# Gating moved to VectorE between the convolution's halves, state products on four column tiles, transposes placed behind halves of the step products

## The chip, the cores and the metric

The program runs on one core of a Trainium2 chip. The time is the device time of one execution in microseconds (us), as the median of several executions. Five engines work side by side and meet through semaphores: TensorE (PE in the profile; PEld is its weight load), VectorE (DVE), ScalarE (ACT), GpSimd (POOL), and SyncE (SP), which issues the DMAs. Each engine takes its own instructions strictly in order.

## The reference

The whole program is a decoder of six layers over x, 8 sequences of 256 tokens with 256 features: x = layernorm(x + layer(x)) six times. The change touches only the first layer, a gated convolution (called `mamba` in the code), and nothing of what it computes:

```python
def _L0_attn_ref(x, W_in, conv_w, conv_b, W_xproj, D, W_out):   # D_STATE = 16
    d_inner, d_conv = conv_w.shape                # 512, 4
    xz = einsum('bld,ed->ble', x, W_in)           # 1024 columns
    xb, z = xz[..., :d_inner], xz[..., d_inner:]
    xpad = pad(xb, d_conv - 1 in front)
    xc = conv_b
    for k in range(d_conv):
        xc = xc + conv_w[:, k] * xpad[:, k:k + L, :]
    xc = silu(xc)
    proj = einsum('bld,ed->ble', xc, W_xproj)     # 16 + 16 + 512 columns
    Bm, Cm = proj[..., :16], proj[..., 16:32]
    delta = softplus(proj[..., 32:])
    bc = einsum('bls,bls->bl', Bm, Cm)
    y = delta * xc * bc[..., None] + D * xc
    y = y * silu(z)
    return einsum('bld,ed->ble', y, W_out)
x = layernorm(x + _L0_attn_ref(...))
```

All data are float32.

## The kernel before

The 2048 tokens are cut into four groups of 512 (two sequences each), numbered by `s`. Inside the layer the features lie on the 128 partitions and the 512 tokens along the free dimension; the 512 inner channels are four chunks of 128, handled in pairs (`c2` is the pair, `c` the chunk). A pair fills one `pair` buffer of PSUM, 128 x 1024 values, two banks. There are three `pair` buffers and two one-bank buffers called `one`.

The functions of one group, in the words of the layer:

- `turn_in(s)`: eight 128x128 transposes of x on PE into two `one` buffers (L88), each copied to SBUF by ACT (L93).
- `project(s)`: four `pair` buffers of four matmuls each (L172). The first two pairs are the channels xb: ACT copies each into the padded tile `xp` (L183), DVE makes the convolution with eight instructions a pair (L187 twice, L192 six times), ACT applies Silu and leaves `xc` (L197). The last two pairs are z: ACT applies Silu from PSUM and leaves `sz` (L178).
- `state(s)`: four matmuls add W_bc's products for the 32 columns B and C into 32 partitions of a `one` buffer (L207). DVE shifts B onto C and multiplies (L212, L214).
- `state_sums`: one matmul with ones adds the 16 products and spreads the sum over all 128 partitions (L219); ACT copies it to `bc` (L221).
- `steps(s, c2)`: eight matmuls (L229) make softplus's argument for one pair; ACT applies Abs (L234) and Exp (L235). `gated` adds ACT's Ln (L240), then DVE takes max(ps, 0) + e (L242), POOL multiplies by `bc` (L243), DVE adds D and multiplies by xc (L246, twice), POOL multiplies by `sz` (L249). The result is `y`. Each of Exp, Ln and Silu is preceded by a load of ACT's function table where it follows another.
- `outputs(s, half, o)`: eight matmuls of y with W_out into a `one` buffer (L259), then the residual sum and layernorm of 256 tokens (`norm`: DVE L103, L110, L111, two small POOL instructions, DVE L116).
- `turn_out(s, half, ps)`: four transposes of the layer's result and ACT's copy (L88, L93), input of the next layer.

The recording layer puts instructions into each engine's order; `tc.issue_after(x)` holds those recorded inside it until after x. A PSUM or SBUF buffer is given to a new tile when its last reader is done. In the order that results, PE's work for one group in the middle is: `state`, `turn_in(s+1)` mixed with the first steps, `steps(s, 0)`, `state_sums`, `steps(s, 1)`, `project(s+1)`, `outputs(s)`, and from s = 1 `turn_out(s-1)` before or in the middle of the next group's first products. After the last `steps` PE goes straight on with the second layer (`cross`), whose first functions are `values` (L342) and `weighted_values` (L361): their PSUM results are copied alternately by ACT (L74) and DVE (L76), and the layer's remaining `outputs(3)` and `turn_out` calls are spread between them.

The loop over the groups:

```python
            for s in range(4):
                bc_p = state(s)
                if s + 1 < 4:
                    turn_in(s + 1)
                e0 = steps(s, 0)
                bc = state_sums(bc_p)
                e1 = steps(s, 1)
                gated(s, 0, *e0, bc)
                gated(s, 1, *e1, bc)
                if s + 1 < 4:
                    last = project(s + 1)
```

## Time and profile before

| what | us | from |
|---|---|---|
| median of three executions | 1465.47 (1463.72 to 1466.76) | times |
| the profiled execution, time | 1460.47 | times |
| the profiled execution, span of its instructions | 1458.0 | page |
| PE busy in the span | 1379.0 (95%) | page, part 1 |
| DVE, ACT, POOL busy | 834.5 (57%), 654.9 (45%), 522.4 (36%) | page, part 1 |
| first layer, PE: first transpose to last step product | 3.72 to 178.6 | timeline of PE |
| PE, DVE, ACT, POOL busy in the first 180 us | 164.8, 87.8, 80.9, 42.3 | table of windows of 20 us |

The matmul records of float32 come in two for each instruction (the timeline shows x16 for eight matmuls of `steps`), so "x16" of L229 in 7.0 us means 0.88 us an instruction. Durations of one engine's successive instructions overlap a little where they do not depend on each other, so sums are best taken from start to start. In the timeline the number in brackets is the engine's idle time before the row, and behind the arrow stands what released it.

### The profile page before, as it was taken

How to read it: one execution, taken by the hardware profiler on the slowest of the kernel's cores; microseconds unless marked ns; L12 is line 12 of the kernel's file. 1: busy time of each engine (PE TensorE's matmuls, PEld its weight loads, DVE VectorE, ACT ScalarE, POOL GpSimd, SP SyncE). 2: the span in 40 equal slices, each digit the busy share in tenths (PEclk: the TensorE clock that was granted, in tenths of full speed). 3: DMA queues.
4: the chain of work that ended last, by engine and by line, in shares of the span. 5: the costliest groups of instructions: out<-in, count | busy, mean ns of one | idle time of the engine just before them, and what ended most of it. 6: DMA issues, size and time to landing. Idle time of an engine off the chain costs nothing.

```text
span 1458.0 us, 21959 instructions
## 1 busy us (share of the span) xinstructions
PE 1379.0 (95%) x7938; PEld 963.7 (66%) x7938; DVE 834.5 (57%) x2285; ACT 654.9 (45%) x1608; POOL 522.4 (36%) x525
## 2 busy tenths in 40 slices
PE   8999889999999999999989999999999999899996
PEld 3443468888885666656566666678888787566564
DVE  3654435564662523323658888835555662787886
ACT  3555342333332112221248877833333322877884
POOL 0333122222210113317435666432343455556541
PEclk9999999999999999999999999999999999999999
DMA  9100023324360012233030000024222210000100
GB/s 236 34 0 1 0 93 93 107 70 156 115 229 15 19 40 87 87 105 105 29 102 1 1 1 2 1 90 123 74 73 82 82 35 9 16 16 16 30 16 16
DMA packets 71679, 87.81 MB, mean 60 GB/s; under 512 B 5588, under 2 KB 66164, under 8 KB 71060
## 3 DMA queue, kind: packets, MB, share of 16 engines
q1 hardware_dynamic: 68164, 77.10, 17.3%
q0 software_dynamic: 3408, 9.31, 2.3%
q8 instruction: 64, 1.05, 0.3%
q14 instruction: 43, 0.35, 0.1%
HBM read 56.87 MB, written 29.52 MB: 59 GB/s over the span
## 4 chain that ended last, share of the span: by engine, by line
PE 75%; DVE 15%; ACT 4%; POOL 3%; issue 3%; DMA 0%; SPq 0%; POOLq 0%; DVEq 0%; ACTq 0%
PE mm L481 9%; PE sc L436 8%; PE mm L737 7%; DVE p L990 6%; PE mm L800 5%; PE op L1027 4%; PE tr L754 4%; PE ps_sc L1012 4%; PE pair L229 4%; PE ps_sc L981 4%; PE sc L399 2%; PE tr L814 2%; PE sc L417 2%; PE sc L465 2%; PE mm L342 2%
## 5 line engine op out<-in xcount | busy, mean ns | idle before, releaser
L997 ACT ACTIVATE p<-p,nmx 128x256 f32<-128x256 f32 x512 | 252.9, 495 | 64.1 <-DVE nmx L990 64.0
L456 POOL TENSOR_TENSOR p<-p,sm 128x616 f32<-128x616 f32 x60 | 72.6, 1216 | 247.4 <-DVE sm L453 217.0
L481 PE MATMUL mm<-Ub,pT 128*128 128x256 f32 (+1 forms) x640 | 144.6, 379 | 0.5 <-ACT pT L74 0.4
L436 PE MATMUL sc<-M,xT_s 128*128 128x308 f32 x512 | 139.6, 423 | 0.8 <-ACT pT L74 0.8
L1012 PE MATMUL ps_sc<-ident,p 128*128 128x128 f32 x1024 | 132.0, 276 | 7.6 <-DVE nmx L990 4.8
L1012 PEld LDWEIGHTS ps_sc<-ident,p 128*128 128x128 f32 x1024 | 113.4, 141 | 34.2 <-issue 13.1
L481 PEld LDWEIGHTS mm<-Ub,pT 128*128 128x128 f32 (+1 forms) x640 | 120.8, 190 | 20.0 <-ACT pT L74 0.9
L737 PE MATMUL mm<-xT_s,w 128*128 128x512 f32 x256 | 115.2, 603 | 2.9 <-DVE h L743 2.1
L436 PEld LDWEIGHTS sc<-M,xT_s 128*128 128x128 f32 x512 | 94.0, 188 | 33.4 <-ACT pT L74 1.5
L449 ACT ACTIVATE p<-p 128x616 f32<-128x616 f32 x64 | 45.8, 716 | 150.0 <-DVE p L445 128.5
L990 DVE CUSTOM_DVE_ANT_0 p<-ps_sc,zero 128x256 f32<-128x256 f32 x256 | 90.7, 421 | 27.6 <-PE ps_sc L981 26.0
L990 DVE CUSTOM_DVE_ANT_0 p<-ps_sc,term 128x256 f32<-128x256 f32 x256 | 90.7, 420 | 27.6 <-PE ps_sc L981 27.5
L997 ACT ACTIVATION_READ_ACCUMULATOR p<-p,nmx 128x1 f32 x512 | 95.8, 187 | 0.0
L774 POOL DMA_INDIRECT xb<-xd,token x39 | 37.2, 954 | 147.3 <-PE tr L781 81.1
L737 PEld LDWEIGHTS mm<-xT_s,w 128*128 128x128 f32 x256 | 48.4, 193 | 58.1 <-issue 53.9
L443 DVE TENSOR_REDUCE nmx<-sc 128x8 f32<-128x616 f32 x64 | 51.1, 799 | 54.2 <-PE sc L436 54.2
L1015 DVE COPY pT<-ps_sc 128x1024 f32<-128x1024 f32 x64 | 77.7, 1214 | 2.7 <-PE ps_sc L1012 2.7
L1015 ACT COPY pT<-ps_sc 128x1024 f32<-128x1024 f32 x64 | 63.7, 996 | 28.8 <-PE ps_sc L1012 28.7
L800 PE MATMUL mm<-wE,xbT 128*128 x156 | 73.5, 593 | 0.3 <-ACT xbT L786 0.3
L741 ACT ACTIVATE g<-mm 128x512 f32<-128x512 f32 x32 | 19.1, 597 | 103.5 <-PE mm L737 99.6
L1027 PE MATMUL op<-pT,va 128*32 128x256 f32 x1024 | 63.4, 386 | 0.0
L452 DVE TENSOR_REDUCE sm<-p 128x8 f32<-128x616 f32 x64 | 50.6, 790 | 22.5 <-ACT p L449 21.9
(287 smaller groups left out, 2654.1 us busy)
## 6 DMA issues: line engine op xcount, KB each, us to landing
Ub<-ud SPq DMA_DIRECT2D x32, 512.0 KB
ud<-U SPq DMA_DIRECT2D x16, 616.0 KB
wE<-in_wE SPq DMA_DIRECT2D x4, 1536.0 KB
yd<-y SPq DMA_DIRECT2D x39, 128.0 KB
Ub<-ud SPq DMA_DIRECT2D x32, 104.0 KB
ud<-U SPq DMA_DIRECT2D x4, 608.0 KB
x_s<-in_x SPq DMA_DIRECT2D x8, 256.0 KB
w<-in_Wo SPq DMA_DIRECT2D x2, 1024.0 KB
```

Of the source, the lines that this page charges most:

```text
L229: nc.tensor.matmul(ps[:, i, :], w_dt[:, kc, c * P : (c + 1) * P], xc[s][kc // 2][:, kc % 2, :], start=kc == 0, stop=kc == 3,)
L436: nc.tensor.matmul(sc[:, a, : 4 * NCTX], xT_b[:, kc, j * P : (j + 1) * P], M[:, a * 4 : a * 4 + 4, kc, at : at + NCTX], start=kc == 0, sto ...
L456: engine.tensor_tensor(pv, pv, bcast(sm, 2, [P, 8, NCTX]), ALU.mult)
L481: nc.tensor.matmul(o[:, j * D : (j + 1) * D], pT[:n, c, j * P : (j + 1) * P],  Us[b][:n, g, c], start=g == 0 and j == 0 and c == 0, stop=g ...
L737: nc.tensor.matmul(ps, w[:, kc, cols], xT_s[:, kc, :], start=kc == 0, stop=kc == 1)
L754: nc.tensor.matmul(o[:, j * D : (j + 1) * D], hs[c][:, at : at + P], w3[:, c, :], start=c == 0, stop=c == 7,)
L800: nc.tensor.matmul(ps, xT[:, kc, :], column(j, kc * 512, 512), start=kc == 0, stop=kc == 1)
L990: self.last = nc.vector.tensor_tensor_reduce(out=p[:, h, :], in0=s4[:, h, :], in1=self.term(b, qb), scale=-1.0, scalar=3.0e38, op0=ALU.add ...
L997: nc.scalar.activation(p[:, h, :], p[:, h, :], AF.Exp, bias=nmx[:, qb, n : n + 1], scale=-1.0, accum_out=sums[:, qb, n : n + 1],)
L1012: nc.tensor.transpose(tr[:, at : at + P], p[:, h, kb * P : (kb + 1) * P], ident)
L1015: (nc.scalar.copy if j else nc.vector.tensor_copy)(self.pT[b, c, j][:, :, :, qb * P : (qb + 1) * P], tr.rearrange("p (h k t) -> p h k t", ...
L1027: nc.tensor.matmul(self.op[b][s * 32 : (s + 1) * 32, c, :], va[:, kb, 8 * c + 2 * s + m, :], self.pT[b, c, s // 2][:, s % 2 * 2 + m, kb, : ...
```

## The change

Four things are changed in the first layer.

1. `state` writes the four chunks' products side by side: each chunk's 32 columns go to a column tile of its own (`tile_position=(0, c * 32)`) and to 32 partitions of its own in half of a `pair` buffer, without adding. ACT copies the 128 x 512 result to `pt`, and a new matmul (`state_products`) with the constant `quarters` (ones where the partition's number modulo 32 is the column's) adds the four parts. The shuffle and the product follow as before, in place. `quarters` is made once by a reduction of the identity on DVE.
2. `gated` does its two multiplications, by `bc` and by `sz`, on DVE. POOL does none of the gating any more. The second pair's gating of group s is recorded inside `project(s + 1)`, between the two halves of the convolution: DVE's order is the first pair's gating, the copy and convolution of the first pair of s + 1, the second pair's gating, the convolution of the second pair.
3. The copy of the first pair into `xp` goes from ACT to DVE (L190); the second stays on ACT.
4. The order on PE: `steps` chains its halves with `issue_after`; `state_products` and `turn_in(s + 1)` come behind `steps(s, 0)`, the transposes between the first products of `steps(s, 1)`; `state_sums` comes between the halves of `steps(s, 1)`; `turn_out(s - 2)` (one group later than before) behind `steps(s, 1)`; `outputs(s)` behind `project(s + 1)`; `state(s + 1)` behind `outputs(s)`.

DMAs, their order on SP, and every engine's order behind the first layer stay as they are, but that `turn_out(1)` now stands right before the second layer's first product.

```diff
-            done, xc, sz, y = [], {}, {}, {}
+            done, xc, sz, y, bc = [], {}, {}, {}, {}
+            quarters = m1.tile([P, 32], F32, name="quarters")
+            nc.vector.tensor_reduce(
+                quarters, ident.rearrange("p (k m) -> p m k", k=4), AX.X, ALU.add
+            )
...
-                    nc.scalar.copy(xp[:, :, 3:], ps.rearrange("p i (b t) -> p (i b) t", b=2))
+                    copy = nc.scalar.copy if c2 else nc.vector.tensor_copy
+                    copy(xp[:, :, 3:], ps.rearrange("p i (b t) -> p (i b) t", b=2))
                     acc = m2.tile([P, 4, SEQ], F32, tag="acc", name="acc")
+                    order = ExitStack()
+                    if c2 == 1 and between:
+                        with tc.issue_after(conv.ins):
+                            order.enter_context(tc.issue_after(between().ins))
...
             def state(s):
-                ps = one()
+                parts = pair()[:, 0, :]
                 for c in range(4):
                     nc.tensor.matmul(
-                        ps[:32, :], w_bc[:, c, :], xc[s][c // 2][:, c % 2, :],
-                        start=c == 0, stop=c == 3,
-                    )
+                        parts[c * 32 : (c + 1) * 32, :], w_bc[:, c, :], xc[s][c // 2][:, c % 2, :],
+                        start=True, stop=True, tile_position=(0, c * 32),
+                    )
+                pt = m1.tile([P, 512], F32, tag="pt", name="pt")
+                nc.scalar.copy(pt, parts)
+                return pt
+
+            def state_products(pt):
+                ps = one()
+                nc.tensor.matmul(ps[:32, :], quarters, pt, start=True, stop=True)
                 sh = m1.tile([32, 512], F32, tag="sh", name="sh")
                 nc.vector.stream_shuffle(sh, ps[:32, :], [(i + 16) % 32 for i in range(32)])
-                bc_p = m1.tile([32, 512], F32, tag="bc_p", name="bc_p")
-                nc.vector.tensor_tensor(bc_p, ps[:32, :], sh, ALU.mult)
-                return bc_p
+                nc.vector.tensor_tensor(sh, ps[:32, :], sh, ALU.mult)
+                return sh
...
             def gated(...):
-                nc.gpsimd.tensor_tensor(t, t, bcast(bc, 1, [P, 2, 512]), ALU.mult)
+                nc.vector.tensor_tensor(t, t, bcast(bc[s], 1, [P, 2, 512]), ALU.mult)
...
-                nc.gpsimd.tensor_tensor(t, t, sz[s][c2], ALU.mult)
                 y.setdefault(s, []).append(t)
+                return nc.vector.tensor_tensor(t, t, sz[s][c2], ALU.mult)
...
             turn_in(0)
-            project(0)
+            last = project(0)
             for s in range(4):
-                bc_p = state(s)
-                if s + 1 < 4:
-                    turn_in(s + 1)
-                e0 = steps(s, 0)
-                bc = state_sums(bc_p)
-                e1 = steps(s, 1)
-                gated(s, 0, *e0, bc)
-                gated(s, 1, *e1, bc)
-                if s + 1 < 4:
-                    last = project(s + 1)
+                with tc.issue_after(last.ins):
+                    pt = state(s)
+                e0, last = steps(s, 0)
+                with tc.issue_after(last.ins):
+                    bc_p = state_products(pt)
+                    if s + 1 < 4:
+                        turn_in(s + 1)
+                e1, last = steps(s, 1, lambda: state_sums(s, bc_p))
+                if s > 1:
                     with tc.issue_after(last.ins):
                         for half in range(2):
-                            outputs(s, half, one())
-                        if s > 0:
-                            for half in range(2):
-                                turn_out(s - 1, half, one())
+                            turn_out(s - 2, half, one())
+                gated(s, 0, *e0)
+                if s + 1 == 4:
+                    gated(s, 1, *e1)
+                else:
+                    last = project(s + 1, lambda: gated(s, 1, *e1))
+                    with tc.issue_after(last.ins):
+                        for half in range(2):
+                            last = outputs(s, half, one())
```

More of the change, by code (lines that the diff above doesn't have):

```diff
@@ L162, in turn_in, with project @@
                     transposed(one(), x_s[:, half * 2 : half * 2 + 2, :], xT_s, half)
-            def project(s):
+            def project(s, between=None):
                 xT_s = xs[s][1]
@@ L191, in project @@
                         for k in range(1, 4):
-                            nc.vector.scalar_tensor_tensor(
+                            conv = nc.vector.scalar_tensor_tensor(
                                 acc[:, two], xp[:, two, k : k + SEQ], cv[:, c, k : k + 1],
@@ L195, in project @@
                             )
+                    order.close()
                     t = m2.tile([P, 2, 512], F32, tag="xc", name="xc", bufs=4)
@@ L214, in state, with state_sums @@
-                nc.vector.tensor_tensor(bc_p, ps[:32, :], sh, ALU.mult)
-                return bc_p
-            def state_sums(bc_p):
+                nc.vector.tensor_tensor(sh, ps[:32, :], sh, ALU.mult)
+                return sh
+            def state_sums(s, bc_p):
                 ps = one()
-                nc.tensor.matmul(ps, ones[:16, :], bc_p[:16, :], start=True, stop=True)
-                bc = m1.tile([P, 512], F32, tag="bc", name="bc")
-                nc.scalar.copy(bc, ps)
-                return bc
@@ L224, in steps @@
-            def steps(s, c2):
-                ps = pair()
+                last = nc.tensor.matmul(ps, ones[:16, :], bc_p[:16, :], start=True, stop=True)
+                bc[s] = m1.tile([P, 512], F32, tag="bc", name="bc")
+                nc.scalar.copy(bc[s], ps)
+                return last
+            def steps(s, c2, between=None):
+                ps, last = pair(), None
                 for i in range(2):
                     c = c2 * 2 + i
-                    for kc in range(4):
-                        nc.tensor.matmul(
-                            ps[:, i, :], w_dt[:, kc, c * P : (c + 1) * P],
-                            xc[s][kc // 2][:, kc % 2, :], start=kc == 0, stop=kc == 3,
-                        )
+                    with tc.issue_after(last.ins) if last else nullcontext():
+                        for kc in range(4):
+                            last = nc.tensor.matmul(
+                                ps[:, i, :], w_dt[:, kc, c * P : (c + 1) * P],
+                                xc[s][kc // 2][:, kc % 2, :], start=kc == 0, stop=kc == 3,
+                            )
+                    if i == 0 and between:
+                        with tc.issue_after(last.ins):
+                            last = between()
@@ L235, in steps, with gated @@
                 nc.scalar.activation(e, e, AF.Exp, scale=-1.0)
-                return ps, e
-            def gated(s, c2, ps, e, bc):
+                return (ps, e), last
+            def gated(s, c2, ps, e):
                 nc.scalar.activation(e, e, AF.Ln, bias=1.0)
@@ L258, in outputs @@
                         at = half * 256 + j * P
-                        nc.tensor.matmul(
+                        last = nc.tensor.matmul(
                             o[:, j * D : (j + 1) * D], y[s][c // 2][:, c % 2, at : at + P],
@@ L264, in outputs @@
                 norm(o, xs[s][0][:, two, :], n_s[:, two, :])
+                return last
             def turn_out(s, half, ps):
@@ L270, in mamba @@
             turn_in(0)
-            project(0)
+            last = project(0)
             for s in range(4):
-                bc_p = state(s)
-                if s + 1 < 4:
-                    turn_in(s + 1)
-                e0 = steps(s, 0)
-                bc = state_sums(bc_p)
-                e1 = steps(s, 1)
-                gated(s, 0, *e0, bc)
-                gated(s, 1, *e1, bc)
-                if s + 1 < 4:
-                    last = project(s + 1)
+                with tc.issue_after(last.ins):
[7 more added lines that the diff above has]
+                if s > 1:
                     with tc.issue_after(last.ins):
                         for half in range(2):
-                            outputs(s, half, one())
-                        if s > 0:
-                            for half in range(2):
-                                turn_out(s - 1, half, one())
+                            turn_out(s - 2, half, one())
[4 more added lines that the diff above has]
+                    last = project(s + 1, lambda: gated(s, 1, *e1))
+                    with tc.issue_after(last.ins):
+                        for half in range(2):
+                            last = outputs(s, half, one())
         return done, [
```

## The prediction

> **What bounds the kernel now.** I read the page first: PE is busy for 95% of the span and holds 75% of the chain that ended last, so a change pays if it takes work or waiting off PE, and costs if PE has to wait for what it moves to another engine. The change lies in the first layer, so I then read who waited for whom in the first 190 us (engine, line, whom it waited for: us in total, times, longest):

> ```profile
> PE one L88 <- DVE r L103: 7.5, 4, 2.0
> PE one L207 <- DVE r L103: 1.9, 1, 1.9
> PE pair L172 <- DVE y L242: 0.7, 3, 0.2
> DVE y L246 <- POOL y L243: 12.3, 5, 2.5
> ```

> PE's real waits inside the layer are for r, the residual sum that empties a `one` buffer of `outputs`: DVE is late with it, because the second half of a convolution and the gating stand before it. The timeline of PE shows where, for the last group (start, duration, row; in brackets the idle time before it and the releaser):

> ```profile
> 131.81 7.03 PE L172 MATMUL pair<-xT_s,w 128*128 128x512 f32 x16
> 139.09 7.13 PE L172 MATMUL pair<-xT_s,w 128*128 128x512 f32 x16 [0.25 <-DVE y L242]
> 146.06 7.07 PE L259 MATMUL one<-w,y 128*128 128x256 f32 x32
> 154.92 0.66 PE L88 MATMUL one<-ident,x_s 128*128 128x128 f32 x4 [1.79 <-DVE r L103]
> 155.41 1.02 PE L229 MATMUL pair<-xc,w 128*128 128x512 f32 x2
> 158.39 0.66 PE L88 MATMUL one<-ident,x_s 128*128 128x128 f32 x4 [1.96 <-DVE r L103]
> 158.98 5.32 PE L207 MATMUL one<-xc,w_bc 128*32 128x512 f32 x8
> 164.22 6.28 PE L229 MATMUL pair<-xc,w 128*128 128x512 f32 x14
> 170.43 1.12 PE L219 MATMUL one<-bc_p,ones 16*128 16x512 f32 x2
> 171.48 7.13 PE L229 MATMUL pair<-xc,w 128*128 128x512 f32 x16
> 178.45 3.74 PE L342 MATMUL mm<-ctxT,w 96*128 96x128 f32 x32
> 184.94 2.00 PE L361 MATMUL sc<-w,VT 64*128 64x256 f32 x16 [2.75 <-ACT VT L74]
> 190.20 3.50 PE L361 MATMUL sc<-w,VT 64*128 64x256 f32 x16 [3.26 <-DVE VT L76]
> ```

> The reader is to see three things. L207, `state`, takes four full-length matmuls for only 32 columns (3.5 us in the other groups). The two waits of nearly 2 us come right behind `outputs`. And L207 takes 5.3 us here: the table of windows gives PE's granted clock as 0.54 from 158.9 to 162.0, so these two waits also cost half speed for some 3.4 us, 1.7 us of work. At the end PE waits twice for the copies of VT, which stand behind the last gating.

> The rows that price the change (group rows: busy, mean ns of one | idle before; the last two are from the timeline of DVE):

> ```profile
> L1027 PE MATMUL op<-pT,va 128*32 128x256 f32 x1024 | 63.4, 386 | 0.0
> L1015 DVE COPY pT<-ps_sc 128x1024 f32<-128x1024 f32 x64 | 77.7, 1214 | 2.7 <-PE ps_sc L1012 2.7
> L456 DVE TENSOR_TENSOR p<-p,sm 128x616 f32<-128x616 f32 x4 | 3.2, 795 | 0.0
> 103.49 0.99 DVE L187 TENSOR_SCALAR acc<-xp,cv 128x512 f32<-128x512 f32 x2
> 104.40 4.05 DVE L192 SCALAR_TENSOR_TENSOR acc<-xp,cv,acc 128x512 f32<-128x512 f32 x6
> ```

> **State products (part 1).** L1027 already runs float32 products on four column tiles: 63.4 us for 1024 records of 256 columns, 62 ns each where one alone shows 386, and in the timeline 32 of them take 1.87 us to the next row. Eight records of 512 columns are half of that, 0.94; I take 1.0 against 3.53, start to start (66.54 to 70.07). [...] Saving 4 x 2.53 = 10.1 us. The new `quarters` matmul is one of L207's kind (3.53 / 4): 4 x 0.9 = 3.6 us on PE. Its input, ACT's copy of 128 x 512 (0.59 as L221), has the 7 us of `steps(s, 0)` to hide in; what follows it (shuffle and product 1.4 us on DVE) has the transposes and half of `steps(s, 1)`, 4.5 us, before `state_sums` asks. Making `quarters` is one small reduction while DVE idles until 13 us: nothing.

> **The waits behind `outputs` (part 4).** They go: now `state` writes a `pair` buffer, and the next `one` is asked for by `quarters`, 8 us after `outputs` end. From 43 us on the timeline lists 0.24, 1.88, 0.25, 1.78, 1.96, 0.25, 1.79, 1.96: 10.1 us, and the half clock at 159, 1.7 us. [...] The windows show the drop right behind them, so I count it. [...]

> What could be late instead: in the changed kernel's instruction order the third `pair` of `project` waits for DVE's new copy of the first, the fourth for ACT's copy of the second, `outputs` for the second gating, `state` for both halves of xc. I count from the end of the first `pair` of `project`, 0. DVE: copy 1.25 (L1015), convolution 4.9 (103.49 to 108.38), gating: max 1.25 (L242 has 1225 ns), multiply, two of L246 1.45 (row 1.42), multiply. The multiply has no row of its size; L456 gives 795 ns for 616 columns, L1015 1214 for 1024, L743 and L103 about 690 for 512, so 1.2 by the slope, 1.25 with hand-over; above, POOL's own 2.35. So gating is 5.2, ends 11.35; the second convolution ends at 16.3, Silu (1.06) at 17.4. PE: three more `pair`s of 3.5, at 10.5; three products of the first y are put first, so the second y is asked for at 11.8; `outputs` end at 17.5, half of `state` at 18.0, when the second xc is asked for. Both come about 0.5 early, and the third `pair` is asked for at 3.5, copy done at 1.3. Without that cover each us more on DVE in this chain is a us on PE, three times. I take no loss. ACT is given `pt` but loses one copy of 1.0 and is at 20 us of work in a round of 39: hidden. POOL keeps only memsets and the two small operations of `norm`; the DVE rows that ran beside it (L187 twice in 3.02 at 93.15, instead of 0.99) get their time back. `turn_in` and `turn_out` keep their numbers; SP and DMAs do not move, and the weights that are now asked for earlier (W_dt at 25 us instead of 28) are issued at 10 us (were they late, it is at most the 3 us, once).

> **The end of the layer.** From the last step product (178.5) to the second L361 is 11.7 us before. After: Abs, Exp, Ln and their two table loads 5.8, two `turn_out` copies that stand between them 1.2, last gating 5.2, copy of VT 0.7: 12.9. But two `turn_out`s of 0.5 have moved from before the last step product to behind it, under this chain. Net 0.2 lost.

> **Sum.** 10.1 - 3.6 + 10.1 + 1.7 - 0.2 = 18.1 us; 17.5 with 0.6 for new hand-overs on PE. Behind the second L361 every engine's order is the same and the chain goes on over PE, so it arrives at the end: 1460.5 - 17.5 = 1443.0 for the profiled execution. The median of the runs shown is 5.0 longer than that execution; carried over, 1448.0.

> **Rivals.** *VectorE becomes the bound.* If a multiply costs POOL's 2.35 instead of 1.25, the chain is 2.2 longer a round; less 0.4 of slack 1.8, three times 5.4, and 2.2 in the last gating: 7.6 lost, 1455.6. For it: the slack is only half a us. Against: every DVE row of that size is near 1.2. *The column tiles run one after another* (other moving data in each tile): 10.1 lost, 1458.1. L1027 has other data in each too. *The ring of `pair` buffers*: were the third `pair` to wait for the second gating's first pass, PE would stop 3.9 us and fall to half clock three times, 3 x 5.6 = 16.8, so 1464.8, no change. The order of instructions shows the wait for the copy, which speaks against it. *Slower:* everything of the gating now stands in one line on DVE, and `outputs` stop for it. The place is the fourth product of `outputs`; a stop of more than 17.5 / 3 = 5.8 us a round (4.1 if each brings 1.7 of half clock) makes the kernel slower, that is DVE's 16.3 us growing to 21 or more. At 1.5 times, as when DVE shares with another engine, the stop is 8.2 - 0.4 + 1.7 = 9.5, three times 28.5: 1476.5. For it: L187 did take three times its time beside POOL; against: POOL is quiet now.

> **Chances.** Forecast 0.81, VectorE bound 0.08, tiles 0.04, ring 0.03, slower 0.04. The forecast's own range is 1443 (the unprofiled runs, 5 us longer, may hold more half clock of this kind) to 1454; to 1458 it takes in most of the first two rivals. 0.2% is 2.9 us, about what the measurement can tell from no change: faster 0.93, same 0.03, slower 0.04.

> **What would show it.** L220 (the new `state`) at 1.0 us for eight records; no wait over 0.5 us on PE between 24 and 160 us; granted clock 1.00 there; the last step product near 159.5, the second L389 (before: L361) near 172.5. Wrong would be: L282 waiting for y L273, L220 for xc L209, or L266 and L273 over 1.4 us.

## The result, and the profile after

The changed kernel takes 1440.54 us (median; 1439.85 to 1446.51) where the kernel before took 1465.43 in the same comparison: 24.9 us less, ratio 0.9845 (95% interval 0.9824 to 0.9866). The forecast was 1448.0 with a range from 1443: the direction was right and the gain too small, and the time lies below the range. The profiled execution takes 1440.51 (span 1438.7), nearly the median itself; before, the profiled execution (1460.47, span 1458.0) was 5.0 shorter than the median shown.

First the order of PE around `state` of the first group, in the second group and at the end of the layer, from its timeline (start, duration, row; in brackets the idle time before the row and its releaser):

```profile
22.32 1.05 PE L220 MATMUL pair<-xc,w_bc 128*32 128x512 f32 x4
23.30 1.98 PE L249 MATMUL pair<-xc,w 128*128 128x512 f32 x4
25.31 1.05 PE L220 MATMUL pair<-xc,w_bc 128*32 128x512 f32 x4
26.29 5.42 PE L249 MATMUL pair<-xc,w 128*128 128x512 f32 x12
...
41.67 13.90 PE L178 MATMUL pair<-xT_s,w 128*128 128x512 f32 x32
55.40 7.24 PE L282 MATMUL one<-w,y 128*128 128x256 f32 x32
62.57 1.22 PE L220 MATMUL pair<-xc,w_bc 128*32 128x512 f32 x8
63.72 7.13 PE L249 MATMUL pair<-xc,w 128*128 128x512 f32 x16
70.79 1.05 PE L230 MATMUL one<-pt,quarters 128*32 128x512 f32 x2
...
163.60 2.05 PE L370 MATMUL mm<-ctxT,w 96*128 96x128 f32 x16 [0.79 <-ACT xT_s L93]
167.27 2.00 PE L389 MATMUL sc<-w,VT 64*128 64x256 f32 x16 [1.62 <-ACT VT L74]
171.79 2.00 PE L389 MATMUL sc<-w,VT 64*128 64x256 f32 x16 [2.52 <-DVE VT L76]
173.72 2.36 PE L427 MATMUL sc<-ctxT,w 96*128 96x154 f32 x16
```

There is no bracket from 7 to 160 us: `outputs` (L282) run into `state` (L220), `state` into the step products. `state` takes 1.15 us from start to start (62.57 to 63.72) where it took 3.53; in the first group it runs in two halves of 0.98. The last step product ends at 159.2 instead of 178.6. The first row that does not belong to the layer or to VT any more is L427 (before: L399), and it starts at 173.72 instead of 193.63: 19.9 us earlier. The rest of the kernel then takes 1265.0 us of span, against 1264.4 before. So the whole difference of the two profiled executions (19.3 of span) lies where the change is.

The timeline of DVE shows the chain on which the forecast hung, in the same group:

```profile
45.30 1.22 DVE L190 COPY xp<-pair 128x1024 f32<-128x1024 f32 x1 [1.54 <-PE pair L178]
...
52.77 1.22 DVE L266 TENSOR_TENSOR y<-y,bc 128x1024 f32<-128x1024 f32 x1
54.03 1.42 DVE L269 SCALAR_TENSOR_TENSOR y<-y,cv,xc 128x512 f32<-128x512 f32 x2
55.48 1.22 DVE L273 TENSOR_TENSOR y<-y,sz 128x1024 f32<-128x1024 f32 x1
```

The two multiplications that had no row before (L266, L273) take 1.22 us each. The chain from the copy to the end of the gating lasts 11.4 us (45.30 to 56.70), forecast 11.35, and PE's timeline shows no wait for it.

### The profile page after: what moved, and what is told of

Same layout as the page of the kernel before. It is cut to its first block, busy times and chain, and to the rows that moved or that the text cites. A ratio compares the mean times of both kernels' runs of the same rounds, so it can differ in the third digit from the quotient of the medians.

```text
span 1438.7 us, 21959 instructions
## 1 busy us (share of the span) xinstructions
PE 1369.4 (95%) x7946; PEld 960.7 (67%) x7946; DVE 846.3 (59%) x2306; ACT 652.0 (45%) x1608; POOL 482.3 (34%) x509
## 4 chain that ended last, share of the span: by engine, by line
PE 78%; DVE 12%; POOL 3%; ACT 3%; issue 3%; DMA 0%; POOLq 0%; SPq 0%; DVEq 0%; ACTq 0%
PE mm L509 9%; PE sc L464 8%; PE mm L765 7%; DVE p L1018 6%; PE mm L828 5%; PE op L1055 4%; PE pair L249 4%; PE pair L178 4%; PE ps_sc L1040 4%; PE ps_sc L1009 4%; PE tr L782 3%; PE sc L427 2%; PE tr L842 2%; PE sc L445 2%; PE sc L493 2%
## 5 line engine op out<-in xcount | busy, mean ns | idle before, releaser
L113 POOL TENSOR_SCALAR rstd<-mv 128x2 f32<-128x2 f32 x48 | 10.7, 224 | 159.3 <-DVE mv L111 158.8
```

## The experiments

Most kernels undo or isolate one part of the change. Executions of both kernels were also traced again, because the median had gained 5 us more than the traces. The names e1 to e18 are used in the tables below.

**The kernel before, again (e1).** No edit.

> The unchanged kernel, for the 5 us between its profiled execution (1460.5, granted clock 0.992) and its other executions (1465.4). Theory A (half-clock stretches): the usual execution has about three more stretches of half clock than the profiled one, each 3.4 us long and worth 1.7 us, most of them behind the waits of nearly 2 us in the first layer; the granted clock of executions near 1465 is then about 0.0035 lower, 0.988 to 0.989. Theory B (something else: DMAs, the chip): executions near 1465 show the same 0.992.

Measured 1460.41 (1459.13 to 1463.35) and 1460.92 for the kernel before beside it, ratio 0.9999 (0.9990 to 1.0008). The executions at 1459 to 1461 have a mean granted clock of 0.990 to 0.992, those over 1462.5 of 0.986 to 0.988. So a kernel's own executions spread by 5 us, and the time goes with the clock; but on this chip the median of before is 1460.4 and 1460.9, not 1465.4.

**Column tiles undone (e2)**, the rest of the change kept:

```diff
-                        parts[c * 32 : (c + 1) * 32, :], w_bc[:, c, :], ...
-                        start=True, stop=True, tile_position=(0, c * 32),
+                        parts[:32, :], w_bc[:, c, :], ...
+                        start=c == 0, stop=c == 3,
...
-                nc.scalar.copy(pt, parts)
-                return pt
+                return parts
...
-                ps = one()
-                nc.tensor.matmul(ps[:32, :], quarters, pt, start=True, stop=True)
+                ps = pt
```

> The changed kernel with state's four products added in place again, as before (no column tiles, no quarters, no copy to pt), all else as changed. If PE without waits is what counts: state 3.5 instead of 1.15 + 0.98, 1.4 us a group, four times 5.6: 1446. If PE still had slack there: 1440.5. If the column tiles also drew in waits: less than 1440.

Measured 1444.04, ratio 0.9880 (0.9864 to 0.9897). Its timeline of PE has the old price back and no wait in the layer:

```profile
63.68 3.62 PE L220 MATMUL pair<-xc,w_bc 128*32 128x512 f32 x8
67.23 7.13 PE L246 MATMUL pair<-xc,w 128*128 128x512 f32 x16
```

The last step product ends at 164.1 in its trace, 4.6 later than the mean of five traces of the changed kernel (159.4), and the row behind VT starts at 179.68, 5.4 later than their mean (174.3). PE's rows give 3 x (3.53 - 1.15) + (3.67 - 1.96) - 4 x 0.98 = 4.9, the second term for the first group, where `state` runs in two halves. The tiles are worth about what PE saves on them, once nothing else waits. The medians alone do not show it: the changed kernel, not run beside this one, took 1440.5 to 1444.3 on other chips.

**Gating ahead of the convolution (e3)**, as before, on VectorE:

```diff
-                    last = project(s + 1, lambda: gated(s, 1, *e1))
+                    gated(s, 1, *e1)
+                    last = project(s + 1)
```

> The changed kernel with the second pair's gating recorded before project, so that it stands on DVE ahead of the copy and both halves of the convolution. If the place between the halves matters: counted from the end of project's first pair, the gating ends at 7.5, the copy at 8.8, and the fourth pair, asked for at 7.0, starts 1.7 late; three groups: 5 us, 1445.7, and more if such a wait brings half clock. If only the engine matters and not the place: 1440.5.

Measured 1452.54, ratio 0.9938 (0.9921 to 0.9954). PE stops at `state`, not at a `pair` of `project` and not for y, in its timeline:

```profile
63.74 1.05 PE L220 MATMUL pair<-xc,w_bc 128*32 128x512 f32 x4
66.28 1.05 PE L220 MATMUL pair<-xc,w_bc 128*32 128x512 f32 x4 [1.49 <-ACT xc L209]
67.27 7.13 PE L249 MATMUL pair<-xc,w 128*128 128x512 f32 x16
```

With the gating first, the convolution of the second pair is what comes late, and `state` stops 1.3 to 1.5 us for xc in each of three groups. With the 0.24 to 0.32 for a `pair` buffer that is 5.1 us of the 8.4 by which the row behind VT starts later (182.71). The wait also splits `state`: without it the two halves take 67.27 - 63.74 - 1.49 = 2.04 us, where four tiles at once take 1.15. That is 0.9 us in each of three groups, most of the rest. Putting the gating between the halves of the convolution is worth about 8 us of trace.

**The multiplications on GpSimd (e4)**, in the changed order:

```diff
-                nc.vector.tensor_tensor(t, t, bcast(bc[s], 1, [P, 2, 512]), ALU.mult)
+                nc.gpsimd.tensor_tensor(t, t, bcast(bc[s], 1, [P, 2, 512]), ALU.mult)
...
-                return nc.vector.tensor_tensor(t, t, sz[s][c2], ALU.mult)
+                return nc.gpsimd.tensor_tensor(t, t, sz[s][c2], ALU.mult)
```

> The changed kernel with the two multiplications of the gating on POOL again, all else as changed. If the engine matters: POOL takes 2.35 each instead of 1.23, the second y comes at 13.8 after the first pair instead of 11.4, outputs ask at 11.8: 2 us of wait in three groups and 2 at the end: 1448.5, with half clock behind the waits up to 1453. If the new order alone made the gain: 1440.5.

Measured 1460.49 (1455.87 to 1465.23), ratio 1.0000 (0.9985 to 1.0016): the whole gain is gone (the profiled execution, 1456.38, is among the fastest of twelve). In its timeline of PE, `outputs` stop for the last multiplication, here in the second group:

```profile
60.78 7.57 PE L282 MATMUL one<-w,y 128*128 128x256 f32 x26 [3.67 <-POOL y L273]
```

The same wait of 3.67 us stands before the rows at 105.22 and 150.53, and each is followed by half clock (from 61.75, 106.12 and 150.50): 3 x (3.67 + 1.7) = 16.1, and the row behind VT starts 17.3 us later than in the changed kernel. I had expected 2 us of wait: the multiplications take 2.59 and 2.72 us here, and DVE is slow beside them (L198 twice 3.04 us instead of 1.00), so the second y comes 15.2 us after the first `pair` and not 13.8. This is the slower rival's mechanism, `outputs` that stop for y with half clock behind each stop, on another engine.

**The changed kernel again (e5)**, and two parts of the change alone on the kernel before, the tiles (e6) and the gating on VectorE (e7), on one chip:

> The changed kernel once more, in several rounds beside the kernel before. Theory A (the true gain is the 19.3 us that the two profiles differ by; the 5 us by which the runs of before lay above its profiled execution belong to the executions of that one comparison): 1440.5 within 1.5, before at 1460 to 1461, ratio 0.985 to 0.9875. Theory B (the gain of the median is 24.9 us, since unprofiled runs of before hold more waits or half clock than the profiled one): before at 1464 to 1466 beside it, ratio 0.983 or less. In both the profile shows the first layer as before: no wait on PE over 0.5 us from 24 to 160 us, no half clock in the first 190 us.

> Before, with the state products on four column tiles, the quarters product and the pair buffer for them, and nothing else of the change: order, gating and copies as before. If the terms of the sum add up as forecast (10.1 less for the tiles, 3.6 more for quarters), 6.5 us less than before: ratio 0.9955, about 1454. If the waits behind the outputs are set by VectorE's lateness and not by which buffer is asked for, they stay or grow by what PE now saves: 1458 to 1461, ratio 0.998 to 1.0. L229 after the turns would then wait for DVE r more than the 2 us of before.

> Before, with both multiplications of the gating on VectorE, in the order of before (both gatings ahead of the convolution), nothing else of the change. If VectorE's lateness with the residual sum comes from its work alone (2.4 us more a pair, 4.9 a group), the waits behind the outputs grow: 1466 or more, ratio 1.004. If it comes from waiting for POOL (12.3 us at L246) and from sharing with it (L187 twice in 3.02 us instead of 0.99), the two balance or better: 1454 to 1459, ratio 0.996 to 0.999.

The first has no edit; the second adds `quarters`, the column tiles and the `pair` buffer to the kernel before; the third is

```diff
-                nc.gpsimd.tensor_tensor(t, t, bcast(bc, 1, [P, 2, 512]), ALU.mult)
+                nc.vector.tensor_tensor(t, t, bcast(bc, 1, [P, 2, 512]), ALU.mult)
...
-                nc.gpsimd.tensor_tensor(t, t, sz[s][c2], ALU.mult)
+                nc.vector.tensor_tensor(t, t, sz[s][c2], ALU.mult)
```

The changed kernel took 1441.65, ratio 0.9849 (0.9825 to 0.9872); here before is at 1465.22, with a mean clock of 0.988. Theory B's number for before came out on this chip, though not its ratio (0.983 or less); theory A's came out on another below. The trace has a step of half clock at 168 us, which neither theory had.

The tiles alone took 1463.42, ratio 0.9976 (0.9961 to 0.9990): 1.8 us instead of the forecast 6.5. The timeline of PE shows two reasons, in the second group and in the last:

```profile
64.39 1.05 PE L211 MATMUL pair<-xc,w_bc 128*32 128x512 f32 x4
66.73 1.05 PE L211 MATMUL pair<-xc,w_bc 128*32 128x512 f32 x4 [1.29 <-ACT xc L201]
67.71 1.12 PE L236 MATMUL pair<-xc,w 128*128 128x512 f32 x2
...
154.81 0.66 PE L88 MATMUL one<-ident,x_s 128*128 128x128 f32 x4 [1.78 <-DVE r L103]
...
158.29 1.12 PE L88 MATMUL one<-ident,x_s 128*128 128x128 f32 x4 [1.41 <-DVE r L103]
```

In the old order `state` never runs in one piece: its records come as four and four or as two and six in every group, and in the second group its halves take 2.03 us beside the wait for xc. With 0.98 for `quarters` that is hardly less than the 3.53 of before. And two waits for r stay in each of the last two groups: PE, which now has less work around them, runs at half clock for three steps before 165 us (one from 111.50, two from 155.87), against one in the first profile of before. The layer's last step product ends at 178.3 as before. The longer waits that I had expected did not come. How much each reason took was not separated.

The gating on VectorE alone took 1457.31, ratio 0.9949 (0.9932 to 0.9965). VectorE has more work there, and is earlier: counted from the group's first L172, the residual sum L103 starts 1.5 us sooner in each of three groups (in the second 63.57 - 42.69 = 20.88 instead of 65.72 - 43.34 = 22.38), since L246 no longer waits for POOL and the six L192 beside POOL's multiplication no longer take 6.15 us (4.06 when POOL is quiet, both in the trace of before). The waits for r fall to, in its view of waits (engine, line, whom for: us in total, times, longest):

```profile
PE one L88 <- DVE r L103: 4.5, 4, 2.0
PE one L207 <- DVE r L103: 0.4, 1, 0.4
```

With the 0.7 for the `pair` buffers that is 5.6 us, instead of 10.1. The two parts alone give 1.8 and 7.9 us, the whole change 23.6 beside them. The rest belongs to the new order on PE and DVE, the moved copy and what the parts do together; neither order nor copy was tried alone. The new order needs the multiplications on VectorE, as without them nothing is gained (e4), but not the tiles, without which 16.9 us of gain stay (e2).

**VT's copies on ACT (e8, e12, e18).** In the first cross product the second L389 waits 2.5 us for a copy of VT, the result of `values`, that DVE can only make behind the last gating. Here ACT makes the copies of VT for the first chunk, and those of U, which follow, but for the last (`early` is true in the first cross product only):

```diff
-    def evac(dst, src):
+    def evac(dst, src, copy=None):
...
+        if copy:
+            return copy(dst, src)
...
+                    nc.scalar.copy if early and c == 0 else None,
...
+                        nc.scalar.copy if early and c == 0 and (g, i2) != (1, 1) else None,
```

> The changed kernel, with the copies of chunk 0 of VT, and of U but for the last, on ACT in the first cross product, so that the second L389 no longer waits for a copy that stands behind the last gating on DVE. If that wait (2.5 us before the second L389) is what holds the end of the layer: 2 to 2.5 us less than the changed kernel, 1438, ratio 0.984 or less. If the weighted values then wait for another copy, or if the next stage waits instead: no change, 1440.5.

> The changed kernel with the copies of VT for chunk 0 on ACT, again. Span times mean clock was 1427.7 against 1429.8 for the changed kernel on the same chip. If that is its gain, and the clock is as in the changed kernel: 1438 to 1440, 2 us below it. If the later layers lose it again by half clock (0.992 against 0.993 last time): 1441 to 1442, no difference.

> The changed kernel with the first copies of VT on ACT, third comparison: the second stage begins at 172.3 in both traces of it and at 173.7 to 175.9 in the four of the changed kernel, so 2.2 us less on the mean if the later layers hold the same half clock: 0.5 us more and 2.6 us less so far in the medians.

The wait is gone; in the timeline of the first of them the sixteen and sixteen records run as one:

```profile
168.70 3.73 PE L393 MATMUL sc<-w,VT 64*128 64x256 f32 x32 [1.62 <-ACT VT L74]
172.36 2.36 PE L432 MATMUL sc<-ctxT,w 96*128 96x154 f32 x16
```

The next stage starts at 172.36, 172.24 and 172.75 in three traces, against 173.53 to 175.92 in five of the changed kernel, 1.8 us less on the mean. The medians were 1442.18, 1439.42 and 1438.37 beside 1441.65, 1442.03 and 1444.27 for the changed kernel on the same chips (ratios to before 0.9849, 0.9851 and 0.9829). The traces say 1.8 us less than the changed kernel; the medians say 0.5 more, 2.6 less and 5.9 less, and the intervals of the ratios overlap each time. That it is faster is likely, and not shown.

**Where the executions differ (e9, e10, e13 to e16).** The kernel before and the changed one, traced again without edits:

> The kernel before, unchanged, one more profiled execution, to find where an execution with a low mean clock loses. Span times mean clock was 1445 for it in 39 executions on two chips, whatever the time, so an execution with clock 0.988 should have a span near 1463, one with 0.991 near 1459. If the half clock that differs between executions stands behind PE's waits in the first layer and the first cross product: clock 0.988 or less shows three or more stretches of half clock before 195 us, 0.991 or more shows two. If it stands in the later layers: those before 195 us are two in both.

> The kernel before once more; as for the last run: with a low mean clock (0.988 or less) three or more stretches of half clock before 195 us if the first layer's waits are what differs between executions, two if the later layers are.

> The kernel before, one more profiled execution. Stretches of half clock before 195 us so far: 2, 3, 3 with clock 0.991 and 0.992, 4 with 0.987. If the low clock of an execution is set there: 0.988 or less goes with four or more before 195 us. If it is set in the later layers: the count before 195 us stays at two or three at any clock.

> The same, one more execution: 0.988 or less with four or more stretches before 195 us if they are set by the first layer's waits, else two or three.

> The same, one more execution: 0.988 or less with four or more stretches before 195 us if they are set by the first layer's waits, else two or three.

> The changed kernel, one more profiled execution on the same chip: none before 160 us, none to two behind the waits for VT near 168 us (0, 1, 2 so far), the later layers as in the kernel before.

Both stated rules failed. Half clock comes in steps of 3.41 us (159.14 to 162.55 in the first profile of before), of which several may follow each other (three from 185.19 in e13). Counted in each trace (the rest is the span from the row behind VT to the end):

| trace | time | clock | steps of half clock before 196 us | row behind VT starts | rest |
|---|---|---|---|---|---|
| before, first profile | 1460.47 | 0.992 | 2 | 193.63 | 1264.4 |
| before, e9 | 1461.47 | 0.991 | 3 | 195.11 | 1264.5 |
| before, e10 | 1463.72 | 0.987 | 4 | 193.65 | 1267.8 |
| before, e13 | 1460.71 | 0.989 | 5 | 195.37 | 1263.0 |
| before, e14 | 1460.80 | 0.991 | 3 | 194.22 | 1264.3 |
| tiles alone, e6 | 1463.69 | 0.986 | 5 | 193.56 | 1268.2 |
| after, first profile | 1440.51 | 0.995 | 0 | 173.72 | 1265.0 |
| after, e11 | 1442.15 | 0.992 | 2 | 175.92 | 1264.4 |
| after, e16 | 1442.10 | 0.990 | 1 | 174.27 | 1266.0 |

The first part differs by some 2 us between executions of one kernel, and the rest by up to 5. The two traces with the lowest clock lose some 3.5 us in the rest. Over seven traces of before (the table's, and e1 and e15 with 195.15 and 194.19) and five of after (e5 and e17 with 173.96 and 173.53) the row behind VT starts at 194.5 and 174.3 on the mean: the change is worth **20.2 us** there, and the rest does not move (1264.7 and 1265.3).

**And the comparison of the medians (e11, e17)**, which these repeat without edits:

> The changed kernel beside the next run. Span times mean clock near 1430 (1430.7 and 1429.8 so far), clock 0.993: 1440 to 1442. No half clock before 160 us in the profile.

> The changed kernel once more in five rounds: the gain of the paired medians was 24.9, 23.6 and 18.4 us, of which 20.0 lie ahead of the second stage of the first cross product by the traces (194.5 before, 174.5 after, means of seven and four traces). Before at 1460.5: gain 18 to 20. Before at 1465: gain 23 to 25, and clock of before 0.988 or less.

| comparison | before (clock) | after (clock) | gain |
|---|---|---|---|
| the first | 1465.43 | 1440.54 (0.994) | 24.9 |
| e5 | 1465.22 (0.988) | 1441.65 (0.993) | 23.6 |
| e11 | 1460.47 (0.991) | 1442.03 (0.992) | 18.4 |
| e17 | 1464.75 (0.988) | 1444.27 (0.992) | 20.5 |

Ratios of e11 and e17: 0.9866 (0.9850 to 0.9881) and 0.9861 (0.9841 to 0.9880). The 4.5 us between the medians of before go with 0.003 of clock, and 0.003 of 1463 us is 4.4. Span times mean clock, averaged over the executions of before, is 1444.5 to 1445.3 us in e1, e5, e11 and e17: the difference between these chips is half clock, and why some chips have more of it is open. e17 missed its expectation. Before is at 1464.75, but the gain is 20.5 and not 23 to 25, as here the changed kernel too has a median 3.5 above its profiled execution (1440.77).

## Why the half clock comes and goes

The windows can be cut finer. In all 18 traces whose stretches of half clock were located, those of one execution start on one grid of 3.413 us, up to the end of the program: in the first profile of before at 159.14, 189.86, 708.69, 1210.45 and 1254.82. From the first to the last of them that is 321 steps of 3.4133 us, and each start is 2.13 or 2.14 more than a multiple of it. In e9 the remainder is 0.33, in e10 1.49, in the first profile of after 3.16. A stretch lasts one step of the grid or several. With the windows laid on that grid, the table of windows of before reads (window, its length, busy time and records of PE, PEld, DVE, ACT, POOL, then PE's granted clock, DMA share and GB/s):

```profile
107.94:111.35 3.41, 1.52 (x6) 0.69 (x6) 2.24 (x7) 1.64 (x2) 1.04 (x3) 1.00 0.00 0
111.35:114.77 3.42, 2.19 (x8) 0.89 (x9) 2.25 (x8) 0.59 (x1) 0.93 (x2) 1.00 0.00 0
```

and that of e9, with the grid 1.8 us earlier:

```profile
109.56:112.97 3.41, 1.45 (x7) 0.56 (x6) 2.24 (x8) 0.52 (x2) 0.93 (x2) 1.00 0.00 0
112.97:116.39 3.42, 3.42 (x5) 0.71 (x5) 0.96 (x5) 0.56 (x1) 0.93 (x2) 0.50 0.00 0
```

The same two waits of 1.8 and 1.96 us stand behind `outputs` at 109 us and again at 155. At 109 in the first profile of before, the window that holds most of them has PE busy for 1.52 us (45%), and the clock stays; in e9 it has 1.45 (42%), and the next window runs at half, where PE's work is stretched to fill it. I laid each trace's grid over it from 20 to 215 us, for the 18 traces together: of 952 windows at full clock, the 22 with PE busy for 43% or less were all followed by half clock. Of the other 930, 7 were, all with PE busy for 46% to 54%: two hold the column tiles of e6, five the products with VT. Another 29 windows from 44% to 54% kept the clock, so the share alone does not decide there.

## Why the prediction was right or wrong

- **State products.** Forecast 1.0 a group. Measured 1.15 in three groups; in the first, where the halves of xc come apart, two halves of 0.98 each (before 3.67, from 23.57 to 25.41 and 25.89 to 27.72). That saves 8.9 us instead of 10.1. `quarters` 0.98 instead of 0.9: 3.9 instead of 3.6. Net 4.9 instead of 6.5, and undoing the tiles confirms the size (4.6 to 5.4).
- **The waits behind `outputs`.** Gone, as forecast, with the half clock at 159. That they cause it is now shown: three waits of 3.67 us at a new place (e4) brought three steps of half clock there, and in the first profile of before the window from 155.73, with PE busy for 1.46 of 3.41 us and the wait of 1.96 in it, is followed by half clock. L207 takes 5.32 us there and 3.62 at 113.17, where the clock stays: these are the 1.7 that were counted.
- **The slack of half a microsecond on VectorE.** The chain was right (11.4 us against 11.35), the slack was not: three `pair`s take PE 10.1 us instead of 10.5, so the second y is asked for at 11.4 and not at 11.8. In the three groups L273 ends at 56.70, 95.78 and 135.73, and the fourth product of `outputs` starts at 56.76, 95.84 and 135.79. PE loses 0.2 us a group at most, but nothing is left over: that the chain still hides was in part luck. What more on it costs, e3 and e4 show: another order of the same work 8 us, POOL's multiplication 17.
- **The end of the layer.** From the last step product to the second L389 12.6 us (12.9 forecast), before 11.6 (11.7).
- **The sum to the second stage of the cross product** was 17.5; the two traces show 19.9, though the tiles bring 1.6 less. Two terms were not in it. The second L361 ran at half clock before (3.50 us) and runs at full clock here (2.00): 1.5 us. I had shown that row and counted only the half clock at 159, so the term of 1.7 should have been 3.2. And the first group's first products took 16.63 us before and 15.50 after, 1.1 us; other traces of before show 15.6 to 16.6 for them, so this is luck and no effect of the change. The last 1.4 us are the 0.6 allowed for hand-overs, which show in no row, and small differences.
- **The step that failed** is the one that carried the sum to the median: "The median of the runs shown is 5.0 longer than that execution; carried over, 1448.0." It makes 5.0 of the 7.5 us by which the forecast was too long; the sum above makes the other 2.5. The 5.0 is no fixed addition: the profiled execution of after is at its median in three comparisons (1440.51 and 1440.54 in the first) and 3.5 below it in e17, and before itself has medians of 1460.5 and 1465 on different chips. What takes its place is half clock that falls differently in each execution, by the grid: mean clock 0.988 in before at 1465, 0.991 at 1460.5, and 0.992 to 0.994 in the changed kernel on every chip. My range had this at its lower end ("may hold more half clock of this kind") and stopped at 1443, as if the profiled sum were exact; the 2.5 us missing in the sum put the result below it. The draw had a part in it: of the four medians of the changed kernel (1440.5, 1441.7, 1442.0, 1444.3) the first is the lowest, and the last lies within the range.
- **Open** is how much of those 5 us belongs to the change. It takes away up to five steps of half clock in the first 196 us, but in the traces of before these cost only up to 2 us more than in its first profile, as those around 190 run into the wait for VT: in e13 the first L361 takes 3.79 us instead of 2.00, the wait behind it shrinks from 3.26 to 1.48, and the row after starts within 1.8 us of the best. In the two traces with the lowest clock the loss lay in the later layers, where the change does nothing. No execution of before at 1465 or more was traced.
- **The rivals** did not happen: L266 and L273 take 1.22 us, the tiles overlap (eight records in 1.15 us instead of 3.53), the third `pair` waits for nobody.

## What to carry to other kernels

Price an engine's waits with what they do to the clock: on this chip a wait of 2 us can cost 1.7 us more (5.32 instead of 3.62 for `state`), a saving between two such waits can be lost (e6: 1.8 us of 6.5 came), and half clock that ends in another wait can cost nothing (e13: the row 1.79 us longer, the wait behind it 1.78 shorter). A profile is one draw of this, so the distance from a profiled execution to the median must not be carried over to a changed kernel as a constant; sum the part that changes, and let the range take the rest. Parts of a change that remove work from the bounding engine, lateness from its supplier, and the order that ties them, can be worth little alone and much more together. And a chain that just hides leaves no room: check both sides of the slack, when the supplier is done and when the other engine asks.

## What the runs showed of the hardware that was not expected

- The grid of 3.413 us above, and the 22 windows, of 952 at full clock in 18 traces, with PE busy for 43% or less: half clock followed each of them.
- Two multiplications of 128 x 1024 moved from POOL to DVE made DVE's own chain 1.5 us a group shorter (e7): beside POOL's two multiplications (2.58 and 2.73 us there, in the trace of before), L187 twice took 3.03 us instead of 1.00 and six L192 6.15 instead of 4.06.
- Eight float32 records of 512 columns on four column tiles took 1.15 us from start to start, 144 ns each, and on one tile 3.53: 3.1 times. Two tiles alone took 0.98 (first group), so `state` split in two halves (2.03 to 2.04 with a wait between them, e3 and e6) loses 0.9 of the 2.4 us.
